# The cross-attention stage of a decoder kernel, issued as turns in program order on five queues

## The chip, the core and the metric

The kernel runs on one core of a Trainium2 chip. The core has a matrix engine (PE, with its weight loads PEld), a vector engine (DVE), a scalar engine (ACT), a general engine (POOL) and a queue that issues transfers (SP); each takes its instructions in order, and they wait for one another by semaphores. The metric is the time of one execution on the device, in microseconds (us). Three runs of the kernel before took 3389.67 to 3397.65 us, with a median of 3396.12.

## The reference

A decoder of two layers on 16 sequences of 128 tokens, 1024 wide, each part followed by an addition and a layer norm: a state-space adapter, a cross-attention, a quantised feed-forward, then a causal attention, a recurrent attention decoder and a binary feed-forward. The change touches the end of the first part and the second:

```python
# end of the adapter (h: its 128-wide result), then norm
h = h @ w_up.T + b_up
x = _layernorm(x + (x_init + h))
# cross-attention, x as (b, c = 128 tokens, n = 1024 columns), ctx as (b, c = 128, m = 256)
q = einsum('oc,bcn->bon', Wq, x)
k = einsum('oc,bcm->bom', Wk, ctx)
v = einsum('oc,bcm->bom', Wv, ctx)
attention = softmax(einsum('bcn,bcm->bnm', q, k) / sqrt(128), axis=-1)
out = einsum('oc,bcn->bon', Wskip, x) + einsum('bnm,bcm->bcn', attention, v)
x = _layernorm(x + out)
```

## The kernel before

The stages follow one another; `stage_cross` comes after `stage_hydra` (the adapter) and before `stage_quant` (the quantised feed-forward). Everything is fp32, and a matrix product of this type is two passes on PE.

For each of the 16 sequences b the stage does, in its source:

- `risen(b)`: the adapter's product, 128 x 1024 in two halves (L526), is added to r (L527), which holds 2x + bias. `Rise.fetch` loads x (L500) and makes r on POOL in two instructions (L502, L503). Then `layer_norm`: sums on DVE (L85 to L89), the reciprocal root on POOL (L95), the normalisation on DVE (L102), written over x. The loop asks for x two sequences ahead; x has 4 buffers and r has 3.
- `context(b)`: loads the context (L534), multiplies it with the folded weight of queries and keys, and with that of values (L536, L538); ACT copies both out (L540).
- `attention(x, kv, i)` for each half i of 512 columns: energies in two pairs (L551), in a ring of three PSUM banks; DVE takes the maximum of each pair (L553) and scales it (L554); ACT makes exponentials and their sums (L557); DVE inverts the sums (L559); POOL multiplies (L560).
- `attended(x, kv, i, ex, r)`: PE transposes the weights (L568), ACT and DVE copy one half each (L570, L572), PE adds the skip product (L575) and the values' products (L577), DVE adds x (L579).
- a second `layer_norm` writes the result over x, and ACT's queue stores it (L597).
- `piece(b)`: one or two of 20 pieces of the next stage's weights: SP loads a chunk (L636, two buffers), ACT rounds it (L621), POOL takes the difference (L622). The first 16 chunks are 128 x 512, the last four 128 x 1024. Sequences 3, 7, 11 and 15 have two pieces each.

The loop issues the next sequence's `risen` and `context` ahead of the second half of the current one. The tile framework schedules these instructions itself: it chooses the order on each queue by priority, and nothing in this stage fixes it. `Ctx.ordered` (L43) fixes it elsewhere: it links each instruction of the engines named to the one before it on the same engine, in the order in which the source issued them. `stage_quant` uses it for four engines, `decoder_scan` for five.

The loads of the next stage (weights L778, x L60) stand on SP's queue behind this stage's, and the weights' space is that of the stage's own buffers.

Of the kernel before, what the change touches and what calls it, by code (L numbers as in the profile page):

```python
# [14 lines left out]
AF = mybir.ActivationFunctionType  # L15
ALU = mybir.AluOpType
AX = mybir.AxisListType
# [6 lines left out]
P = 128  # L24
NB = 16
# [73 lines left out]
def layer_norm(K, pool, src, dst):  # L99

    mv, ve = norm_sums(K, pool, src)
    K.nc.vector.tensor_scalar(dst, src, mv[:, 0:1], norm_root(K, pool, ve), ALU.subtract, ALU.mult)  # L102
# [372 lines left out]
class Rise:  # L475
# [14 lines left out]
    def fold(self, bank):  # L490
# [3 lines left out]
        w["kq"] = K.t(self.pool, [P, P], "wkq")  # L494
        nc.scalar.copy(w["kq"], pw)

    def fetch(self, b):
        K, nc = self.K, self.K.nc
        x = K.t(self.pool, [P, HID], "x", bufs=4)
        nc.sync.dma_start(x, K.a["x"][b])  # L500
        r = K.t(self.pool, [P, HID], "r", bufs=3)
        nc.gpsimd.tensor_tensor(r, x, self.bup, ALU.add)  # L502
        nc.gpsimd.tensor_tensor(r, x, r, ALU.add)  # L503
        self.got.append((x, r))


def stage_cross(K, rise, xmid, dst, piece):

    nc, a = K.nc, K.a
    scale = 1.0 / math.sqrt(128.0)
    w = rise.w
    with ExitStack() as st:
        work = K.pool(st, "c_work", 2)
        ps = K.pool(st, "c_ps", 1, PSUM)

        def risen(b):

            x, r = rise.got[b]  # L520
            if b + 2 < NB:
                rise.fetch(b + 2)
            for i in range(2):
                cols = slice(i * 512, (i + 1) * 512)
                pu = K.t(ps, [P, 512], "pu")
                nc.tensor.matmul(pu, xmid[:, b * P:(b + 1) * P], w["up"][:, cols], start=True, stop=True)  # L526
                nc.vector.tensor_tensor(r[:, cols], pu, r[:, cols], ALU.add)  # L527
            layer_norm(K, work, r, x)
            return x

        def context(b):

            cx = K.t(work, [P, DC], "cx", bufs=3)
            nc.sync.dma_start(cx, a["ctx"][b])  # L534
            pk = K.t(ps, [P, 2, DC], "kv")
            nc.tensor.matmul(pk[:, 0, :], w["kq"], cx, start=True, stop=True)  # L536
            for mc in range(2):
                nc.tensor.matmul(pk[:, 1, mc * P:(mc + 1) * P], cx[:, mc * P:(mc + 1) * P], w["v"], start=True, stop=True)  # L538
            kv = K.t(work, [P, 2, DC], "kv_s")
            nc.scalar.copy(kv, pk)  # L540
            return kv

        def attention(x, kv, i):

            ex = K.t(work, [P, 4, DC], "ex")
            sm = K.t(work, [P, 4], "sm")
            for h in range(2):
                pe = K.t(ps, [P, 2, DC], "e", bufs=3)
                for j in range(2):
                    m = 4 * i + 2 * h + j  # L550
                    nc.tensor.matmul(pe[:, j, :], x[:, m * P:(m + 1) * P], kv[:, 0, :], start=True, stop=True)  # L551
                nm = K.t(work, [P, 2], "nm")
                nc.vector.tensor_reduce(nm, pe, AX.X, ALU.max)  # L553
                nc.vector.tensor_scalar(nm, nm, -scale, None, ALU.mult)  # L554
                for j in range(2):
                    m = 2 * h + j
                    nc.scalar.activation(ex[:, m, :], pe[:, j, :], AF.Exp, bias=nm[:, j:j + 1], scale=scale, accum_out=sm[:, m:m + 1])  # L557
            rs = K.t(work, [P, 4], "rs")
            nc.vector.reciprocal(rs, sm)  # L559
            nc.gpsimd.tensor_tensor(ex, ex, rs.unsqueeze(2).to_broadcast([P, 4, DC]), ALU.mult)  # L560
            return ex

        def attended(x, kv, i, ex, r):
            at = K.t(work, [P, 2, 4, P], "at")
            for mc in range(2):
                pt = K.t(ps, [P, 4, P], "t", bufs=2)
                for j in range(4):
                    nc.tensor.transpose(pt[:, j, :], ex[:, j, mc * P:(mc + 1) * P], K.ident)  # L568
                if mc == 0:
                    nc.scalar.copy(at[:, 0], pt)  # L570
                else:
                    nc.vector.tensor_copy(at[:, 1], pt)  # L572
            cols = slice(i * 512, (i + 1) * 512)
            po = K.t(ps, [P, 512], "o")
            nc.tensor.matmul(po, w["skip"], x[:, cols], start=True, stop=False)  # L575
            for mc in range(2):
                nc.tensor.matmul(po, kv[:, 1, mc * P:(mc + 1) * P], at[:, mc].rearrange("p a b -> p (a b)"),  # L577
                                 start=False, stop=(mc == 1))
            nc.vector.tensor_tensor(r[:, cols], po, x[:, cols], ALU.add)  # L579


        x, kv = risen(0), context(0)
        ex = attention(x, kv, 0)
        for b in range(NB):
            r = K.t(work, [P, HID], "ro")
            for i in range(2):
                if i == 0 and b + 1 < NB:
                    x1, kv1 = risen(b + 1), context(b + 1)
                nxt = None
                if i == 0:  # L590
                    nxt = attention(x, kv, 1)
                elif b + 1 < NB:
                    nxt = attention(x1, kv1, 0)
                attended(x, kv, i, ex, r)
                ex = nxt
            layer_norm(K, work, r, x)
            nc.scalar.dma_start(dst[b], x)  # L597
            piece(b)
            x, kv = (x1, kv1) if b + 1 < NB else (None, None)

# [16 lines left out]
def parts(K, hi, lo, v, eng):  # L619

    K.nc.scalar.copy(hi, v)  # L621
    eng.tensor_tensor(lo, v, hi.bitcast(F32), ALU.subtract)  # L622


def quant_weights(K, slab, stage):

    nc, a = K.nc, K.a
    w, todo = {}, []
    for n, k, m in (("gate", 8, FFI), ("up", 8, FFI), ("down", 4, HID)):
        w[n] = [K.t(slab, [P, k, m], f"w_{n}{i}", F32R) for i in range(2)]  # L630
        todo += [(n, c, m) for c in range(k)]

    def piece(b):
        for n, c, m in todo[b * len(todo) // NB:(b + 1) * len(todo) // NB]:
            raw = K.t(stage, [P, m], "raw")
            nc.sync.dma_start(raw, a[f"ff_w_{n}T"][c * P:(c + 1) * P, :])  # L636
            parts(K, w[n][0][:, c, :], w[n][1][:, c, :], raw, nc.gpsimd)
    return w, piece


def quant_vectors(K, keep):
# [669 lines left out]
class Front:  # L1311
# [131 lines left out]
    def biased(self, t, q):  # L1443
        sl = slice(q * 256, (q + 1) * 256)
        self.nc.vector.tensor_tensor(self.x[t][:, sl], self.x[t][:, sl], self.W["la_yyb"][:, sl], ALU.add)
# [19 lines left out]
    def normed(self, t, h):  # L1465
        sl = slice(h * 512, (h + 1) * 512)
        self.nc.vector.tensor_scalar(self.x[t][:, sl], self.r[t][:, sl], self.mv[:, 0:1], self.rs, ALU.subtract, ALU.mult)
# [446 lines left out]
```

## Time and profile before

| what | us |
|---|---|
| median of three runs | 3396.12 |
| the profiled execution, device time | 3398.38 |
| its span, first to last instruction | 3396.6 |
| first product of the adapter in the stage (L526) | 309.9 |
| last normalisation (L102) starts | 584.5 |
| last store issued (L597) | 585.4 |
| loads of the next stage issued (L778, L60) | 588.1 to 593.0 |
| first use of them (ACT, L671) | 600.8 |

The starts of L102 for the adapter's result, by sequence:

| b | 0 | 1 | 2 | 3 | 4 | 5 | 6 | 7 |
|---|---|---|---|---|---|---|---|---|
| us | 318.3 | 326.1 | 346.1 | 366.9 | 385.4 | 405.4 | 428.0 | 442.9 |

| b | 8 | 9 | 10 | 11 | 12 | 13 | 14 | 15 |
|---|---|---|---|---|---|---|---|---|
| us | 458.9 | 473.1 | 488.5 | 502.7 | 518.3 | 532.6 | 548.1 | 562.4 |

How to read the profile: it records one execution. A group of instructions is named by its line in the kernel and its engine; "x<-r" means that x is written and r is read. A wait is put down to the semaphore that came last. A matrix product's end is modelled. The granted clock of PE is a share of its full rate.

### The profile page before, as it was taken

The page shows a single profiled execution, that of the slowest core. Times are in us where ns is not written, and L with a number is a line of the kernel's source. Part 1 is how long each engine was busy: PE and PEld are TensorE (multiplying, and loading weights), DVE is VectorE, ACT ScalarE, POOL GpSimd, SP SyncE. Part 2 cuts the span into 40 slices and gives each one's busy share as a digit, 9 for nine tenths or more (in the row PEclk, how much of TensorE's full clock was granted, in tenths as well). Part 3 has the DMA queues.
Part 4 walks back from the last instruction along what each step waited for, and adds up shares of the span by engine and source line. Part 5 has one row for each costly group of instructions (what it writes and reads, how often), then busy time and mean ns, then how long its engine had stood idle before and what let it go on. Part 6 is the DMA issues. An engine that isn't in the chain of part 4 may idle for free.

```text
span 3396.6 us, 62991 instructions
## 1 busy us (share of the span) xinstructions
PE 3080.5 (91%) x24917; PEld 1671.7 (49%) x24917; DVE 1858.2 (55%) x5180; ACT 1443.7 (43%) x3642; POOL 904.3 (27%) x1087
## 2 busy tenths in 40 slices
PE   7887887788899999999998999999999999999998
PEld 3444454677455545555553444444444444444465
DVE  5765686688144544545243455555555555555555
ACT  3443333432032323324123555555555555555533
POOL 3333764566233233332011111111111111111122
PEclk8887899999899999898999999999999999999999
DMA  5001321211410100103312000100010000000144
GB/s 195 1 1 30 110 82 71 80 69 63 151 38 13 50 25 19 44 25 100 99 57 80 11 29 24 30 24 30 24 30 23 24 17 24 17 17 14 32 127 103
DMA packets 97215, 170.22 MB, mean 50 GB/s; under 512 B 14362, under 2 KB 55194, under 8 KB 96922
## 3 DMA queue, kind: packets, MB, share of 16 engines
q1 hardware_dynamic: 92858, 157.10, 14.5%
q10 hardware_dynamic: 4064, 9.11, 0.7%
q8 instruction: 197, 3.23, 0.4%
q14 instruction: 96, 0.79, 0.1%
HBM read 115.83 MB, written 51.64 MB: 49 GB/s over the span
## 4 chain that ended last, share of the span: by engine, by line
PE 61%; ACT 10%; DVE 9%; POOL 6%; issue 4%; DMA 1%; SPq 0%; POOLq 0%; DVEq 0%; ACTq 0%
PE p L841 8%; ACT th L1132 8%; PE s L1223 8%; PE pf L1117 7%; PE p L912 6%; PE p L1060 3%; PE m L1672 3%; PE gq L1259 3%; PE ff L1238 2%; PE t L890 2%; PE s L869 2%; POOL xs L675 2%; PE p L854 2%; PE ff L1136 2%; PE s L1167 2%
## 5 line engine op out<-in xcount | busy, mean ns | idle before, releaser
L1132 ACT ACTIVATE th<-pf 128x512 f32<-128x512 f32 x512 | 264.3, 602 | 277.0 <-PE pf L1117 276.9
L878 ACT ACTIVATE s<-s,nm 128x128 f32<-128x128 f32 x512 | 198.2, 389 | 251.6 <-DVE nm L875 221.4
L1252 POOL COPY hist<-gT 128x16 f32<-128x16 f32 x256 | 42.4, 197 | 935.3 <-DVE gT L1250 935.3
L1223 PE MATMUL s<-hb,aD 128*32 128x256 f32 x4096 | 276.1, 387 | 0.6 <-DVE aD L1211 0.6
L912 PE MATMUL p<-ga_Wo,cT 128*128 128x512 f32 x512 | 228.7, 595 | 0.0
L1205 ACT COPY pf<-enc 128x512 f32<-128x512 f32 x381 | 224.6, 589 | 8.1
L841 PE MATMUL p<-xT,ga_Wq 128*128 128x512 f32 x512 | 226.4, 597 | 0.0
L881 POOL TENSOR_TENSOR s<-s,rs 128x512 f32<-128x512 f32 x128 | 133.1, 1039 | 325.1 <-DVE rs L880 317.3
L1117 PE MATMUL pf<-R,waf 32*128 32x160 f32 x2032 | 181.4, 426 | 33.8 <-DVE R L1275 33.8
L841 PEld LDWEIGHTS p<-xT,ga_Wq 128*128 128x128 f32 x512 | 95.4, 190 | 113.8 <-issue 111.0
L912 PEld LDWEIGHTS p<-ga_Wo,cT 128*128 128x128 f32 x512 | 93.8, 190 | 113.8 <-issue 111.7
L1141 DVE TENSOR_REDUCE nm<-s 128x1 f32<-128x128 f32 x128 | 37.3, 292 | 203.6 <-PE s L1136 203.6
L1223 PEld LDWEIGHTS s<-hb,aD 128*32 128x32 f32 x4096 | 106.8, 109 | 84.2 <-DVE aD L1211 45.7
L1243 ACT ACTIVATE fs<-ff,rx 128x384 f32<-128x384 f32 x127 | 73.9, 582 | 173.1 <-DVE rx L1241 171.5
L1136 PE MATMUL s<-th,vaE 128*32 128x128 f32 x2048 | 109.0, 286 | 36.3 <-ACT th L1132 28.1
L892 DVE COPY pT<-t 128x512 f32<-128x512 f32 x128 | 87.9, 687 | 92.5 <-PE t L890 92.3
L95 POOL TENSOR_TENSOR ln_rs<-ln_ve,neghalf 128x1 f32<-128x1 f32 x64 | 37.8, 595 | 345.0 <-DVE ln_ve L89 345.0
L1117 PEld LDWEIGHTS pf<-R,waf 32*128 32x128 f32 x2032 | 79.4, 182 | 99.3 <-DVE R L1275 74.0
L1136 PE MATMUL ff<-th,vaE 128*32 128x128 f32 x2048 | 109.6, 287 | 16.2
L1060 PE MATMUL p<-xT,qT 128*128 128x512 f32 x256 | 115.8, 606 | 0.3 <-ACT qT L1055 0.2
L913 DVE TENSOR_TENSOR xr<-p,xr 128x512 f32<-128x512 f32 x32 | 22.1, 692 | 168.8 <-PE p L912 168.8
L869 PE MATMUL s<-kT,qT 32*128 32x128 f32 x1024 | 107.7, 312 | 0.0
(394 smaller groups left out, 6787.5 us busy)
## 6 DMA issues: line engine op xcount, KB each, us to landing
x<-x SPq DMA_DIRECT2D x79, 512.0 KB, 3.6
xt<-xT SPq DMA_DIRECT2D x8, 1024.0 KB, 7.4
x<-x ACTq DMA_DIRECT2D x16, 512.0 KB, 2.6
xr<-x SPq DMA_DIRECT2D x16, 512.0 KB, 3.6
x<-xr SPq DMA_DIRECT2D x16, 512.0 KB, 2.6
x<-x SPq DMA_DIRECT2D x128, 64.0 KB, 2.3
xb<-r SPq DMA_DIRECT2D x16, 512.0 KB, 3.0
xb<-xb SPq DMA_DIRECT2D x16, 512.0 KB, 4.0
```

The source lines that it names most:

```text
L841: nc.tensor.matmul(pq, lhsT, xT[:, k].rearrange("p i t -> p (i t)"), start=(k == 0), stop=(k == 7))
L869: nc.tensor.matmul(psc[n][:, r, :], qT[sl, 4 * kc + r, i, :], kT[sl, kc, i, :], start=True, stop=True)
L878: nc.scalar.activation(s[:, r, :], s[:, r, :], AF.Exp, bias=nm[:, r:r + 1], accum_out=sm[:, r:r + 1])
L881: nc.gpsimd.tensor_tensor(s, s, rs.unsqueeze(2).to_broadcast([P, 4, P]), ALU.mult)
L912: nc.tensor.matmul(po, cT[:, k, :], w["o"][h][:, k, :], start=(k == 0), stop=(k == 7))
L1060: nc.tensor.matmul(py, xT[:, k, b % 4, :], ys[:, k, :], start=(k == 0), stop=(k == 7))
L1117: nc.tensor.matmul(pf[:, k, first:first + n].rearrange("p b t -> p (b t)"), lhs[32 * k:32 * k + 32, :], rhs[32 * k:32 * k + 32, 32 * first ...
L1132: nc.scalar.activation(th.rearrange("p i (k t) -> p i k t", t=32), pf[:, :, 4 * g:4 * g + 4, :].rearrange("p k i t -> p i k t"), AF.Tanh)
L1136: nc.tensor.matmul(pe[32 * i:32 * i + 32, :], D["va"][:, 31 - b:63 - b], th[:, i, :], start=False, stop=(g % 2 == 1), skip_group_check=True)
L1205: nc.scalar.copy(pf[:, k], D["enc"][:, k])
L1223: nc.tensor.matmul(pg[32 * i:32 * i + 32, :], aD[:, 4 * g + i, :], D["hb"][:, 4 * g + i, :], start=(g == 0), stop=(g == 3), skip_group_che ...
L1259: nc.tensor.matmul(gq[32 * q:32 * q + 32, :], gT[:, c].rearrange("p e b -> p (e b)"), D["gs"][:, c, q * P:(q + 1) * P], start=False, stop= ...
```

## The change

The stage's helpers are split into steps, and one loop issues them as turns from b = -1 to 16: in turn b, the second energies of sequence b, the adapter's product, norm and context of b + 1, both value products of b, the first energies of b + 1, and what is left of b - 1 (its last addition, sums, norm and store). `K.ordered` then holds this order on PE, DVE, ACT, POOL and SP. The norm's root is written in place. The maxima have 4 buffers instead of 2, the small tiles of the norm 3 instead of 2. The store is issued by SP instead of ACT. `quant_weights` gives two functions: `fetch`, which loads, and `piece`, which rounds; the loads of a turn's piece are issued at the end of the turn before it. x is loaded three sequences ahead, and the context two.

```diff
+    def load_x(self, b):
+        x = self.K.t(self.pool, [P, HID], "x", bufs=4)
+        self.K.nc.sync.dma_start(x, self.K.a["x"][b])
+        self.got.append([x])
+
+    def biased(self, b):
+        self.got[b].append(self.K.t(self.pool, [P, HID], "r", bufs=3))
+        x, r = self.got[b]
+        self.K.nc.gpsimd.tensor_tensor(r, x, self.bup, ALU.add)
+
+    def doubled(self, b):
+        x, r = self.got[b]
+        self.K.nc.gpsimd.tensor_tensor(r, x, r, ALU.add)
...
+        def root(key):
+            nc.gpsimd.tensor_tensor(VE[key], VE[key], K.neghalf, ALU.pow)
+
+        def normed(dst, v, key):
+            nc.vector.tensor_scalar(dst, v, MV[key][:, 0:1], VE[key], ALU.subtract, ALU.mult)
...
+        def maxima(b, i, h):
+            nm = PE[b, i, h, "nm"] = K.t(work, [P, 2], "nm", bufs=4)
+            nc.vector.tensor_reduce(nm, PE[b, i, h], AX.X, ALU.max)
+            nc.vector.tensor_scalar(nm, nm, -scale, None, ALU.mult)
...
+        def weighted(b, i):
+            nc.gpsimd.tensor_tensor(EX[b, i], EX[b, i], SM[b, i].unsqueeze(2).to_broadcast([P, 4, DC]), ALU.mult)
...
-        x, kv = risen(0), context(0)
-        ex = attention(x, kv, 0)
-        for b in range(NB):
-            r = K.t(work, [P, HID], "ro")
-            for i in range(2):
-                if i == 0 and b + 1 < NB:
-                    x1, kv1 = risen(b + 1), context(b + 1)
-                nxt = None
-                if i == 0:
-                    nxt = attention(x, kv, 1)
-                elif b + 1 < NB:
-                    nxt = attention(x1, kv1, 0)
-                attended(x, kv, i, ex, r)
-                ex = nxt
-            layer_norm(K, work, r, x)
-            nc.scalar.dma_start(dst[b], x)
-            piece(b)
-            x, kv = (x1, kv1) if b + 1 < NB else (None, None)
+        order = K.ordered((mybir.EngineType.PE, mybir.EngineType.DVE, mybir.EngineType.Activation, mybir.EngineType.Pool,
+                           mybir.EngineType.SP))
+        context_load(0)
+        context_load(1)
+        rise.load_x(2)
+        piece[0](0)
+        for b in range(-1, NB + 1):
+            now, back, soon, far = 0 <= b < NB, 0 <= b - 1, 0 <= b + 1 < NB, 2 <= b + 2 < NB
+            if back:
+                added(b - 1, 1)
+            if now:
+                energies(b, 1)
+                maxima(b, 1, 0)
+                exps(b, 1, 0)
+                piece[1](b)
+            if soon:
+                rest = rise_half(b + 1, 0)
+            if now:
+                maxima(b, 1, 1)
+                exps(b, 1, 1)
+            if soon:
+                rest()
+            if now:
+                turned(b, 0)
+                copied(b, 0, 0)
+            if back:
+                sums(RO[b - 1], (b - 1, "o"), 1)
+            if soon:
+                sums(R[b + 1], (b + 1, "x"), 0)
+                rest = rise_half(b + 1, 1)
+            if far:
+                rise.biased(b + 2)
+            if soon:
+                rest()
+                sums(R[b + 1], (b + 1, "x"), 1)
+                variance((b + 1, "x"))
+                root((b + 1, "x"))
+                context(b + 1)
+            if now:
+                over(b, 1)
+                copied(b, 0, 1)
+                weighted(b, 1)
+            if soon:
+                normed(X[b + 1], R[b + 1], (b + 1, "x"))
+            if back:
+                variance((b - 1, "o"))
+                root((b - 1, "o"))
+            if now:
+                attended(b, 0)
+                added(b, 0)
+            if soon:
+                energies(b + 1, 0)
+                maxima(b + 1, 0, 0)
+                exps(b + 1, 0, 0)
+            if back:
+                normed(X[b - 1], RO[b - 1], (b - 1, "o"))
+                nc.sync.dma_start(dst[b - 1], X[b - 1])
+            if far:
+                rise.doubled(b + 2)
+            if now:
+                turned(b, 1)
+                copied(b, 1, 0)
+            if soon:
+                maxima(b + 1, 0, 1)
+                exps(b + 1, 0, 1)
+            if now:
+                copied(b, 1, 1)
+                attended(b, 1)
+                sums(RO[b], (b, "o"), 0)
+            if soon:
+                over(b + 1, 0)
+                weighted(b + 1, 0)
+            if 0 <= b and b + 3 < NB:
+                rise.load_x(b + 3)
+            if 0 <= b and b + 2 < NB:
+                context_load(b + 2)
+            if soon and 0 <= b:
+                piece[0](b + 1)
+        order()
...
+    came = {}
+
+    def fetch(b):
+        for n, c, m in todo[b * len(todo) // NB:(b + 1) * len(todo) // NB]:
+            raw = came[n, c] = K.t(stage, [P, m], "raw")
+            nc.sync.dma_start(raw, a[f"ff_w_{n}T"][c * P:(c + 1) * P, :])
+
     def piece(b):
         for n, c, m in todo[b * len(todo) // NB:(b + 1) * len(todo) // NB]:
-            raw = K.t(stage, [P, m], "raw")
-            nc.sync.dma_start(raw, a[f"ff_w_{n}T"][c * P:(c + 1) * P, :])
-            parts(K, w[n][0][:, c, :], w[n][1][:, c, :], raw, nc.gpsimd)
-    return w, piece
+            parts(K, w[n][0][:, c, :], w[n][1][:, c, :], came[n, c], nc.gpsimd)
+    return w, (fetch, piece)
```

## The prediction

> **What bounds the kernel now.** I read the page first (PE busy 91% of the span, but no stage is named there), then the stage alone: it runs from the adapter's first product at 309.9 us to the last store at 585.4. Stretches of 15 us show two regimes (columns: us, then busy us of PE, PEld, DVE, ACT and POOL, granted PE clock, DMA share, GB/s):
>
> ```profile
> 390.00:405.00 15.00, 12.52 (x49) 7.79 (x47) 8.78 (x19) 5.09 (x11) 14.04 (x8) 0.93 0.20 73
> 465.00:480.00 15.00, 14.70 (x59) 9.02 (x58) 13.06 (x29) 6.19 (x23) 9.56 (x7) 1.00 0.22 79
> ```
>
> In the first, POOL is the full engine: the scheduler put all 20 weight pieces ahead, and they are over at 401.6. From sequence 7 on, the norm of the adapter's result (L102) comes at 442.94 and, eight sequences later, at 562.38: 14.93 us each. From sequence 0 (318.26) to 7 it is 17.8 us each. PE's own work for one sequence is 12.8 us, from starts that follow one another at full clock: a 512-column product takes 0.86, a 256-column one 0.43 (adapter 1.72, context 0.86, energies 3.4, skip and values 5.1), eight transposes 0.85 (1.7). So 2 us a sequence are idle even in the good part.
>
> The waits of the stage (engine and line, whom it waited for, us, times, longest) say who is late:
>
> ```profile
> ACT ex L557 <- DVE nm L554: 66.4, 37, 6.3
> DVE x L102 <- POOL ln_rs L95: 24.7, 11, 4.6
> ```
>
> L554 is a scaling of 128x2 numbers. Its durations are 113 ns at least and 2072 at most. The timeline (start, us) shows why:
>
> ```profile
> 412.39 2.35 POOL L502 TENSOR_TENSOR r<-x,bup 128x1024 f32<-128x1024 f32 x1
> 414.81 2.34 POOL L503 TENSOR_TENSOR r<-x,r 128x1024 f32<-128x1024 f32 x1
> ```
> ```profile
> 412.79 1.98 DVE L554 TENSOR_SCALAR nm<-nm 128x2 f32<-128x2 f32 x1
> ...
> 415.28 1.91 DVE L554 TENSOR_SCALAR nm<-nm 128x2 f32<-128x2 f32 x1
> ```
>
> Both end with POOL's instruction (414.77 and 417.19 against 414.74 and 417.15), and DVE's queue stands behind them. L102 is of the same kind. Last, the chain of waits in the good part (start, us):
>
> ```profile
> 472.20 0.82 DVE x L102
> ...
> 473.04 2.61 DMA x<-x
> ...
> 475.73 3.37 DMA x<-x
> ...
> 479.16 1.58 POOL r L502
> ```
>
> The store of one sequence frees the buffer into which x of a later one is loaded, and POOL waits for that.
>
> **The change, part by part.** The instruction counts stay: the same products, reductions, copies and 20 pieces. What changes is the order on five queues, and one store queue. I write one turn with R as zero: the moment at which POOL has the adapter's root of sequence b+1.
>
> *DVE and PE after R.* The norm starts 0.04 later (pair at 442.05) and takes 0.81: 0.85. First energies of b+1 start 0.14 later (as at 459.82): 0.98. The maximum starts 1.17 after them (482.58 to 483.75) and takes 0.60, with its scaling: 2.85. POOL's next is `weighted` of the second half (1.89). Does it take the port before the norm? This is the unknown price of the change. In all eight places where two roots follow one another, the L102 that waits for the first starts 0.07 after the second has begun and still runs its 0.81; where a long instruction follows, there is one row:
>
> ```profile
> 345.67 1.49 POOL L622 TENSOR_TENSOR w_up<-raw,w_up 128x512 fp32r<-128x512 f32 x1
> ```
> ```profile
> 346.11 1.60 DVE L102 TENSOR_SCALAR x<-r,ln_mv,ln_rs 128x1024 f32<-128x1024 f32 x1
> ```
>
> There L102 lost, but POOL had begun 0.44 ahead of it; and POOL, which had met the earlier L102 for 0.37 us, lost only 0.22, so that it wants the port some 0.15 after its start. By that the norm wins at 0.07, and costs POOL about 0.73 instead. The rule of the Trainium skill (SBUF — State Buffer, Who interferes with whom) speaks against the change: the shared port pair is an exclusive lock, whoever issues first holds it for the whole instruction, and here POOL's next instruction is queued ready at the very moment at which DVE must first see the root. Taken so, the norm ends at 1.89 + 0.55 = 2.4, not 0.85. By the row a turn pays nothing, by the rule 1.55 and what follows. I take the row.
>
> So `weighted` ends at 2.58, the root of the finished sequence b-1 at 3.09, its norm at 3.94 (again ahead of POOL's `doubled`). `doubled` (2.35 + 0.75 lost) then ends at 6.15, and the scaling of the second maximum, ready at 4.5, stands behind it until 6.17; so does the copy of the transposed half (6.80), for which the last values wait: PE 6.85 to 7.70. The second energies start there, their first maximum is scaled at 9.54, the exponentials end at 10.6.
>
> *SP.* The store goes from ACT's queue to SP's, and SP now carries, in this order, store of b-1, x of b+3, context, raw piece. x of b+3 takes the buffer of b-1, so it waits for the store to land, and the piece is queued behind it. From the norm at 3.94: store issued and landed 2.7 (473.04 to 475.73), x issued at 6.65, two issues of 0.4 later the piece at 7.45. A piece alone lands in 2.7, one issued 1.7 us behind an x in 3.1 (370.73); for 0.8 us behind x and context I take 3.8, between 2.7 and 4.5 (all 896 KB at the rate between the 256 and 512 KB rows). It lands at 11.25. On ACT its copy (0.63, 0.05 to start) comes next: 11.93. On POOL, 0.05 later, the piece's difference (1.27), then `biased` (2.31), then the root (0.52): 16.07. **A turn is 16.1 us.** Without the wait on the piece, ACT would have been free at 10.6 and the turn 15.4; without any port wait PE's copies would allow 13.8. On ACT the second pair of exponentials stands behind the piece, ends at 12.9, and DVE's reciprocal, copy and norm stand behind that; they are ready at 14.6, before 16.07.
>
> *Sum.* First root at 317.2 as before (316.62 + 0.55). Turn 0 has its inputs: after a table load (1.28 on ACT, as before) `weighted` starts at 323.5, then piece, `biased` and root on POOL (1.89 + 1.27 + 2.31 + 0.52): 329.5. Turn 1 has its loads early, and no norm of b-1 stood ahead of `doubled`: exponentials at 10.3, then 4.7 of copy and POOL as above, 15.0: 344.5. Turns 2 to 12: eight of 16.1 = 128.8, three with two pieces (one more 1.27 on POOL) 17.35 = 52.05. Turn 13 carries a `down` piece: copy 1.05, difference 2.35, landing 0.6 more: 18.2. Turn 14 has no `biased` and no x ahead of its piece (10.6 + 0.05 + 1.05 + 2.35 + 0.55): 14.6. Together 558.15 for the root of sequence 15. Behind it the end is like that of before: last two pieces, `weighted`, transposes, values, norm: 22.05 (before, 562.38 to 584.52: 22.1). The last norm starts at 580.2 instead of 584.52: 4.3 us earlier. What follows (last store, weights, first loads of the next stage) hangs on that store in both. Nothing else pays: buffers for maxima go from 2 to 4, 16 store issues of 0.33 leave an ACT that is busy 6 of 15 us; if that cover goes, they cost at most 5.3 us in all, and here they leave.
>
> The profiled execution took 3398.4 (span 3396.6); minus 4.3 is 3394.1. The median of the runs is 2.3 lower, so 3391.8.
>
> **A second rule.** TensorE: Matmul & The Clock Gate (What's actually happening) has the clock halve after an idle window of some 3.4 us. In the trace the clock is 0.75 to 0.93 in four of the stretches before 420 us and 1.00 from 435 to 585. My turn leaves PE 3.3 us idle, in gaps up to 1.5 us: by the row at 1.00 it keeps its clock. Were the rule to bite, first energies take 3.4 instead of 1.7, of which the maximum sees 0.85 a turn, 10 us in all.
>
> **The rivals.**
>
> *POOL wins the port* (slower). Place: the norm right after each root. It ends at 2.4; energies follow at 2.54; the root of b-1 is done at 3.06 and `doubled` runs to 5.33, ahead of the scaling that is ready at 4.31. So the norm of b-1 ends at 6.16, not 3.94, and the whole SP chain with it: 6.16 + 12.15 = 18.3 a turn. With turn 1 at 346, eight of 18.3, three of 19.55, then 20.4, 16.2, and 22.3 for the end, the last norm comes at 610: 25.4 later, **3421**. It decides as soon as POOL takes the port within 0.07 of its start; a loss at `doubled` alone gives 18.0. Over 16.4 us a turn the stage is slower than before. For it: the L622 row. Against: the eight pairs.
>
> *The pieces and the port don't bind* (faster). If pieces land by 10.6, turns are 15.4: 8.4 less, 3383; if scalings slip between POOL's instructions too, 13.8: 27.6 less, 3364. Centre 3374. For it: the good part of before has 14.9 a sequence in a worse order. Against: SP's queue is strictly behind the store.
>
> *The order is not kept* is no rival of weight: the built order on all five queues is the written one.
>
> **How the numbers follow.** A measurement tells 0.3% (10.2 us) from no change; same is 3386 to 3406. Forecast, 3392 (own range 3384 to 3402): 0.40, of it 0.06 faster, 0.28 same, 0.06 slower. Port lost, 3405 to 3435: 0.38, 0.01 same, 0.37 slower. Fast, 3362 to 3386: 0.22, 0.20 faster, 0.02 same. Sum: 0.26, 0.31, 0.43. With both signs holding much, the range goes to both: 3370 leaves out 0.08, 3428 leaves out 0.09.
>
> **What would show it.** Step by step: the L102 of adapter norms 16.1 us apart in turns with one piece; each 0.81 long and 0.04 behind its root (1.6 to 2.4 means the port was lost); ACT's copy of a piece waiting for its DMA; SP waiting for its store; L554's successor held by `doubled` once a turn. It is wrong if PE stays busy (13 us apart), or if the stretch to the next stage's first load changes by more than a few us.

## The result, and the profile after

The changed kernel takes **3429.2 us** (median of four runs, 3425.77 to 3430.7) against 3396.89 for the kernel before in the same comparison: 1.0098 times, 95% interval 1.0080 to 1.0116. It is slower by about 32 us; the forecast was 3392.

The profiled execution has a span of 3428.0 us, 31.4 more than before. I cut it at two points that both kernels have: the adapter's first product of the stage and the first use of the next stage's loads on ACT. Before, the stretch between them is 309.94 to 600.77, 290.8 us; after, 307.55 to 634.75, 327.2 us: 36.4 longer. What lies outside is 5.0 shorter. The outside part varied by up to 19 us over the executions shown below, whatever the edit, so the length of the stage is a sharper measure than the whole time; it is given for every kernel.

The waits of the changed stage (311 to 620 us; engine and line, whom it waited for, us, times, longest):

```profile
ACT ex L589 <- DVE nm L584: 170.9, 31, 9.1
...
PE e L579 <- DVE ln_mv L548: 41.5, 14, 4.3
```

L584 is the scaling that was L554 before (66.4 us there). PE's wait for L548 is new: L548 is only the last instruction that ended, behind the norm (L556) in DVE's queue. Of SP's own waits in the same stretch, this one belongs to the loads of x (L499):

```profile
SPq L499 <- DMA x<-x: 27.9, 12, 2.7
```

What it waits for, 12 times, is the store that frees the buffer, as the prediction had it. Now the place where the root of the next sequence comes (timeline; start, us, engine, line):

```profile
439.99 0.56 POOL L553 TENSOR_TENSOR ln_ve<-ln_ve,neghalf 128x1 f32<-128x1 f32 x1
...
440.51 1.90 POOL L596 TENSOR_TENSOR ex<-ex,sm 128x1024 f32<-128x1024 f32 x1
440.58 2.37 DVE L556 TENSOR_SCALAR x<-r,ln_mv,ln_ve 128x1024 f32<-128x1024 f32 x1 [0.53 <-POOL ln_ve L553]
...
443.86 2.35 POOL L509 TENSOR_TENSOR r<-x,r 128x1024 f32<-128x1024 f32 x1
...
444.97 1.26 DVE L584 TENSOR_SCALAR nm<-nm 128x2 f32<-128x2 f32 x1
446.15 0.80 DVE L556 TENSOR_SCALAR x<-ro,ln_mv,ln_ve 128x1024 f32<-128x1024 f32 x1
```

POOL's `weighted` (L596) begins 0.07 us before the norm, and the norm takes 2.37 us instead of 0.81: it ends 0.54 after L596. All 15 adapter norms that have `weighted` behind their root take 2.37. Then `doubled` (L509) holds the scaling (L584), which ends at 446.23, 0.02 after `doubled`. The norm of sequence b-1 stands behind that scaling on DVE; it is not in a race of its own here. It starts 5.55 to 5.57 us after the adapter's norm in every full turn. The chain of waits of one turn shows what this norm sets off (start, us, what):

```profile
461.38 2.37 DVE x L556
...
463.89 1.21 PE e L579 x4
...
465.85 1.16 DVE nm L584
467.01 0.73 DVE x L556
...
467.76 2.60 DMA x<-x
...
471.33 3.37 DMA raw<-ff_w_upT
...
474.72 0.63 ACT w_up L723
...
475.42 1.27 POOL w_up L724
...
478.95 0.56 POOL ln_ve L553
...
479.54 2.37 DVE x L556
```

Read it as a circle: norm, energies, maximum, scaling, norm of b-1, its store, SP's next issues, the landing of the weight piece, its copy and difference, `biased`, the root, and the next norm. It closes in 18.16 us. The starts of the adapter's norm are 18.17 to 18.81 apart in the eight turns with one piece, 19.81 to 20.79 with two, and the last norm starts at 618.75 instead of 584.52.

### The profile page after: what moved, and what is told of

It is laid out like the page before. It is cut to its first block, busy times and chain, and to the rows that moved or that the text cites. A ratio compares the mean times of both kernels' runs of the same rounds, so it can differ in the third digit from the quotient of the medians.

```text
span 3428.0 us, 62998 instructions
## 1 busy us (share of the span) xinstructions
PE 3082.9 (90%) x24917; PEld 1674.0 (49%) x24917; DVE 1875.7 (55%) x5180; ACT 1441.3 (42%) x3642; POOL 897.9 (26%) x1087
## 3 DMA queue, kind: packets, MB, share of 16 engines
q1 hardware_dynamic: 95162, 165.49, 14.9%
## 4 chain that ended last, share of the span: by engine, by line
PE 60%; ACT 10%; DVE 9%; POOL 5%; issue 4%; DMA 2%; SPq 0%; POOLq 0%; ACTq 0%; DVEq 0%
PE p L948 8%; ACT th L1239 8%; PE s L1330 7%; PE pf L1224 7%; PE p L1019 6%; PE p L1167 3%; PE m L1779 3%; PE gq L1366 3%; PE ff L1345 2%; PE t L997 2%; PE s L976 2%; PE p L961 2%; POOL xs L782 2%; PE ff L1243 2%; PE s L1274 2%
## 5 line engine op out<-in xcount | busy, mean ns | idle before, releaser
L589 ACT ACTIVATE ex<-e,nm 128x256 f32<-128x256 f32 x128 | 59.5, 471 | 170.9 <-DVE nm L584 170.9
L1243 PE MATMUL ff<-th,vaE 128*32 128x128 f32 x2048 | 109.6, 286 | 16.3
L579 PE MATMUL e<-kv_s,x 128*128 128x256 f32 x256 | 75.2, 446 | 47.2 <-DVE ln_mv L548 41.5
```

The lines of the kernel that those rows point to most:

```text
L1243: nc.tensor.matmul(pe[32 * i:32 * i + 32, :], D["va"][:, 31 - b:63 - b], th[:, i, :], start=False, stop=(g % 2 == 1), skip_group_check=True)
```

## The experiments

Three theories were open. **Port:** the norm's wait behind `weighted` costs the time by itself. **Circle:** the turn is the chain shown above, and what matters is only what shortens it. **Scaling:** the held scaling on ACT's way is what costs. The table has the two kernels and the twelve edits; e1 to e11 are edits of the changed kernel, e12 of the one before. "Turn" is the distance of two adapter norms with one piece and with two, where the pattern is regular (turns 2 to 12). Where the piece stands at the turn's end (e4, e5, e8, e10), the longer distance comes one turn later. "Late" in the rows of before and e12 is the mean from sequence 7 to 15. Ratios are to the kernel before, with their 95% intervals.

| kernel | median us | ratio | stage us | turn, 1 piece | 2 pieces |
|---|---|---|---|---|---|
| before | 3394.9 to 3398.3 | 1 | 290.8 | 14.9 late, 17.8 early | |
| after | 3429.20 | 1.0098 [1.0080, 1.0116] | 327.2 | 18.2 to 18.8 | 19.8 to 20.8 |
| e1 | 3428.26 | 1.0097 [1.0082, 1.0113] | 321.9 | 18.2 to 18.9 | 20.2 to 20.6 |
| e2 | 3435.34 | 1.0116 [1.0100, 1.0132] | 324.5 | six of 17.6, 18.6, 19.6 | 19.1 to 19.9 |
| e3 | 3411.99 | 1.0046 [1.0031, 1.0061] | 303.4 | 16.6 to 16.8 | 18.2 to 19.1 |
| e4 | 3409.64 | 1.0044 [1.0027, 1.0061] | 301.6 | 16.9, once 17.2 | 17.3 |
| e5 | 3410.16 | 1.0043 [1.0024, 1.0062] | 299.9 | 17.1, once 16.8 | 17.1 |
| e6 | 3410.54 | 1.0042 [1.0028, 1.0056] | 307.4 | 17.0 to 17.3 | 18.2 |
| e7 | 3412.12 | 1.0042 [1.0024, 1.0061] | 306.4 | 16.8 late, 16.3 to 25.6 early | |
| e8 | 3375.83 | 0.9938 [0.9917, 0.9959] | 272.6 | 15.3 | 16.1 |
| e9 | 3425.25 | 1.0078 [1.0059, 1.0098] | 321.7 | 18.0 to 18.7 | 19.4 to 20.6 |
| e10 | 3371.07 | 0.9918 [0.9896, 0.9939] | 265.7 | 14.8 | 14.8 |
| e11 | 3426.26 | 1.0080 [1.0062, 1.0099] | 315.8 | 17.6 to 18.0 | 18.9 to 20.4 |
| e12 | 3391.93 | 0.9980 [0.9972, 0.9988] | 281.0 | 14.4 late, 16 to 21 early | |

Before ran in each of the four comparisons; its four medians are given, and each ratio is to the runs of the same comparison.

### e1: the norm of the next sequence ahead of `weighted`

```diff
             if now:
-                over(b, 1)
                 copied(b, 0, 1)
-                weighted(b, 1)
             if soon:
                 normed(X[b + 1], R[b + 1], (b + 1, "x"))
+            if now:
+                over(b, 1)
+                weighted(b, 1)
```

> DVE's reciprocal of the sums moves behind the norm of b+1, so that POOL has nothing ready when it has the root. Cycle theory (a turn is one closed chain: root, norm, first energies, maximum and scaling, norm of b-1, store, load of x, piece, its copy and difference, biased, root; a lost port costs only what it adds to that chain): the norm falls from 2.37 to 0.81 us, but `doubled` now starts right behind the root of b-1 and takes the port from the norm of b-1, which ends 6.4 us after the root as before: turns stay at 18.2 to 18.6, time 3424 to 3431. Port theory (each lost port at the root costs its 1.55 us in each of 14 turns, wherever it falls): 22 us less, 3407.

All adapter norms take 0.81 us now, and the time is that of the changed kernel. The timeline of one turn says where the gain went:

```profile
440.93 0.81 DVE L556 TENSOR_SCALAR x<-r,ln_mv,ln_ve 128x1024 f32<-128x1024 f32 x1 [2.44 <-POOL ln_ve L553]
...
444.37 2.35 POOL L509 TENSOR_TENSOR r<-x,r 128x1024 f32<-128x1024 f32 x1
444.44 2.83 DVE L556 TENSOR_SCALAR x<-ro,ln_mv,ln_ve 128x1024 f32<-128x1024 f32 x1 [0.51 <-POOL ln_ve L553]
```

The same race is lost at the next place: `doubled` begins 0.07 before the norm of b-1, which takes 2.83 and ends 447.27. That is 6.34 after the first norm's start, where the changed kernel has 6.37 (446.95 less 440.58). The circle is as long as before. The port theory, that the adapter's norms cost 22 us by themselves, falls.

### e2: `doubled` at the turn's end

```diff
-            if far:
-                rise.doubled(b + 2)
             if now:
                 turned(b, 1)
...
                 weighted(b + 1, 0)
+            if far:
+                rise.doubled(b + 2)
```

> POOL's `doubled` moves from the middle of the turn to its end, behind `weighted` of the next first half. Cycle theory: the norm of b+1 still takes 2.37, but the first scaling and the norm of b-1 no longer stand behind `doubled`: the norm of b-1 ends 5.3 instead of 6.4 us after the root, 1.1 less in each of 12 turns, 3415. Port theory: nothing changes at the root, 3429. If `doubled` at its new place holds up the scalings of the second energies: slower than 3429.

Most turns became shorter (17.6), but the time did not: 3435.34, 20 over the expectation. The stage is 2.7 us shorter than in the changed kernel and the rest of this execution 10.5 us longer, so half of the miss lies outside the stage and is not explained. Inside it, the moved instruction now holds another scaling, that of the second energies, for 1.90 us (0.17 when free), and the piece's copy comes late behind it.

### e3: both moves

> Both edits together. Cycle theory: the norm of b+1 takes 0.81, the norm of b-1 ends 4.35 us after the root instead of 6.4: turns of 16.5 us with one piece, 25 us less, 3404; more than the two edits give one by one (0 and 14). Port theory: 22 us less, as with the first edit alone, 3407.

Both norms take 0.81 us, and 24 us are gone from the stage. As far as the norms go, this is what my forecast assumed: its turn was to be 16.1 and is 16.6 to 16.8. It is not the forecast's order, since `doubled` stands at the turn's end here. The time, 3412, is 8 above the expectation. The timeline shows the port at work in a third place:

```profile
446.19 2.35 POOL L509 TENSOR_TENSOR r<-x,r 128x1024 f32<-128x1024 f32 x1
446.30 2.26 DVE L584 TENSOR_SCALAR nm<-nm 128x2 f32<-128x2 f32 x1
```

### e4: the piece at the turn's end

```diff
             if now:
-                piece[1](b)
...
                 weighted(b + 1, 0)
+            if now:
+                piece[1](b)
```

> ACT's copy and POOL's difference of a piece move from the head of the turn to its end; the chunk is loaded a turn ahead of that. The norms lose the port as in the changed kernel. Cycle theory: store, load of x and piece leave the chain, the root waits for its sums instead, 1.5 us less in single turns and more in those with two pieces: 25 us less, 3404. Port theory: 3429. A theory that only the extra length of two-piece turns matters: 3 times 1.3 to 2 us, 3424.

Here the piece's copy and difference stand behind the turn's last `weighted`, and SP is no longer in the chain of waits of a turn. The norms keep their 2.37 us, yet 25.6 us leave the stage, and turns with one and two pieces are nearly equal. The wait for the piece was part of what set the turn. What is left in the chain of one turn are the norm and two held scalings:

```profile
469.10 2.37 DVE x L556
...
473.49 1.28 DVE nm L584
...
480.02 0.80 DVE nm L584
...
481.53 0.70 DVE r L538
```

This edit moves three things at once, the landing, ACT's copy and POOL's difference; e6 moves the transfer alone.

### e5: all three moves

> The changed kernel with all three moves: VectorE's part of the second energies of b and its weights behind the norms of b+1 and b-1, the doubled difference at the turn's end, and the piece of the next weights at the turn's end. If the cycle of the turn is what costs (norm, store, load and piece were one part of it, the roots and the doubled difference on GpSimd another), both parts are gone from in front of the root and the norms take 0.81 us; what is left in the way is that the scale of the second energies stands behind the doubled difference or the piece on GpSimd. Then a turn is about 15.95 us (16.85 less 0.9), and the kernel 12 us under the one with the late piece alone: 3398. If only the port of the norm costs, 14 norms of 1.56 us are gone and nothing else: 22 us less than the changed kernel, 3407. If the place of the piece alone matters, the time is that of the kernel with the late piece, 3410.

Missed by 12 us: no better than e3 or e4 alone. The timeline shows the new holder of the circle:

```profile
440.07 2.35 POOL L509 TENSOR_TENSOR r<-x,r 128x1024 f32<-128x1024 f32 x1
440.54 1.90 DVE L584 TENSOR_SCALAR nm<-nm 128x2 f32<-128x2 f32 x1
...
443.58 0.68 DVE L538 TENSOR_TENSOR r<-pu,r 128x512 f32<-128x512 f32 x1
```

With `doubled` and the piece at the end of the turn, the first scaling of the second energies is held for 1.90 us, and with it all that DVE has behind it, the next maximum and the adapter's addition (L538) first. What was won at the norms is paid at the scalings.

### e6: the piece's fetch ahead of the store on SP

```diff
+            if soon and 0 <= b:
+                piece[0](b + 1)
             if back:
                 normed(X[b - 1], RO[b - 1], (b - 1, "o"))
                 nc.sync.dma_start(dst[b - 1], X[b - 1])
...
-            if soon and 0 <= b:
-                piece[0](b + 1)
```

> The changed kernel with one move on SP: the fetch of the piece (8 KB into the staging buffer) stands ahead of the store of sequence b-1 and of the load of x behind it, all else unchanged. If the chain norm of b-1, store, load x, piece, difference, root is the cycle, its middle (2.6 us of store, the load's issue and 3.4 us of landing) falls out, and the next limit is GpSimd's own order: turns of about 17.1 us with one piece and 18.4 with two, some 19 us less than the changed kernel: 3410. If SP's order is not in the cycle (the port of the norm or GpSimd's total is), the time stays at 3429. The norm of the next sequence stays at 2.37 us in either case.

It hit: turns of 17.0 to 17.3 and 18.2, 3410.5. Nothing else differs; the norms still take 2.37. (A piece of 128x512 is a transfer of 256 KB in the trace, not 8 KB.) In the chain of waits the store, the load of x and the landing are gone, and the circle runs through scaling, exponentials and the piece's copy instead:

```profile
464.12 2.38 DVE x L556
...
468.51 1.28 DVE nm L584
...
475.33 0.80 ACT ex L589 x3
...
476.94 1.28 POOL w_up L724
...
480.49 0.56 POOL ln_ve L553
```

This is the one-move test of the forecast's part on SP: the order of the transfers alone is worth 19 us of the 32. It does not say that the races are worth only the other 13: e3 takes 24 us out of the same stage and leaves SP's order as it is.

### e7: the same steps without the fixed order

```diff
-        order()
```

> The changed kernel without the order fence behind each turn: the same steps, in the same program order, but the scheduler may place each step by its own priorities on each engine, as in the kernel before. If the fixed order costs the time (pieces spread over the turns, behind SP's store and GpSimd's roots), it falls back to about the time of the kernel before: 3391 to 3403. If the steps themselves cost it (stores on SP, the second energies split from the first, roots in place), it stays at 3415 or more.

Between the two: 3412, and the stage 15.5 us longer than before's. So neither answer is right alone: some 21 us of the stage's 36.4 go with the fixed order, and the rest with the steps as they are written, even when the scheduler may place them. The chain of its late turns has, one behind the other,

```profile
460.78 1.44 DVE nm L584
...
462.81 1.84 DVE nm L584
```

two held scalings, 3.3 us of a turn of 16.8. In which part the split steps, the store on SP and the buffers caused this order was not tried.

### e8: all three moves, and a scaling that the port doesn't hold

```diff
-            nc.vector.tensor_scalar(nm, nm, -scale, None, ALU.mult)
+            for j in range(2):
+                nc.vector.tensor_scalar(nm[:, j:j + 1], nm[:, j:j + 1], -scale, None, ALU.mult)
```

> The kernel with all three moves, and the scale of the maxima (128x2) done as two 128x1 operations, of which none in the traces so far was held by GpSimd (135 to 156 ns each, against 1.2 to 1.9 us of a held 128x2). If the scale's wait for the port is what is left in the cycle, a turn falls to GpSimd's own sum, about 14.9 us, and the kernel to 14 us under the one with all three moves: 3384. If that wait is not in the cycle, it is the same within 3 us, or a little slower by 32 more instructions. If the 128x1 form is held by GpSimd as well, its rows show 1 us or more, and the time is the same.

The two 128x1 instructions take 0.21 to 0.22 us together and are not held, though they start 0.11 us after a long instruction of POOL:

```profile
469.08 2.36 POOL L509 TENSOR_TENSOR r<-x,r 128x1024 f32<-128x1024 f32 x1
469.19 0.21 DVE L585 TENSOR_SCALAR nm<-nm 128x1 f32<-128x1 f32 x2
```

Against e5 the stage is 27 us shorter and the time 34; it is 0.6% faster than before. What the time gained beyond that lies outside the stage, where the edit changes no instruction, so 27 is the safer figure. Turns are 15.3 where 14.9 were expected, but the time undercut its number (3376 against 3384). The edit brought 27 us or more on top of e5 and not 14: the held scalings were a larger part of e5's circle than I had put down. The circle now runs through POOL and the sums:

```profile
460.62 0.81 DVE x L556
...
461.68 1.89 POOL ex L597
...
469.08 2.37 POOL r L509
...
471.48 0.69 DVE r L538
```

Here `doubled` (L509) ends just ahead of the adapter's addition that reads its result (L538): no port, a dependence.

### e9: the divided scaling alone

> The changed kernel with one edit: the scaling of the maxima (128x2) as two 128x1 operations. If the scaling's wait for the port is what the change costs, every turn loses one wait of 1.0 to 1.3 us, 17 us in all, as the same edit brought 34 us on top of the three moves: 3395 to 3412. If the cycle norm, store, load, piece, root decides, the norm of b-1 still stands behind the doubled difference on GpSimd, so turns stay at 18.2 and the time at 3424 to 3430: the edit is worth something only once the other two parts are out of the way.

Worth 4 us in the time, at the edge of what can be told from nothing (the intervals of e9 and the changed kernel overlap), and turns stay at 18 us and more. The same edit takes 27 us from the stage when the rest of the circle is short (e8 against e5), and 5.5 here. The theory that the scalings alone cost the time falls.

### e10: both roots together, both norms together

```diff
                 root((b + 1, "x"))
                 context(b + 1)
+            if back:
+                variance((b - 1, "o"))
+                root((b - 1, "o"))
...
                 normed(X[b + 1], R[b + 1], (b + 1, "x"))
+            if back:
+                normed(X[b - 1], RO[b - 1], (b - 1, "o"))
+                nc.sync.dma_start(dst[b - 1], X[b - 1])
             if now:
                 over(b, 1)
                 weighted(b, 1)
+            if far:
+                rise.doubled(b + 2)
```

(on top of e8; the four steps leave their later places)

> All three moves and the divided scaling (3376), and GpSimd's order changed once more: both roots one after the other, both norms one after the other on VectorE, and the recip of the second half with its weights behind both, then the doubled difference in the middle of the turn again. The trace of the kernel before this edit has turns of 15.3 us in which the chain runs root, norm, weights 1.89, root, norm, two maxima, weights 1.89, doubled difference 2.36, adapter sums, root. With the edit the doubled difference and one pair of weights leave that chain; GpSimd's own sum is 12.2 us, the products' 13.8. If that chain is the cycle, turns are 13.8 to 14.2 and the kernel about 3357. If PE or ScalarE binds already, it stays at 3376; if the doubled difference in the middle holds up a norm again, norms show 2 us or more and the time is above 3376.

The best kernel of the study: 3371.07, 0.8% under the kernel before. All turns are 14.8 us, with one piece or two. Over e8 it is not told apart (their intervals overlap); the stage is 6.9 us shorter. The turn missed 13.8 to 14.2, and the chain says why:

```profile
460.84 1.07 POOL ln_ve L553
...
463.00 1.90 POOL ex L597
...
464.95 1.09 PE t L604 x8
...
468.62 1.73 PE e L579 x8
...
472.08 1.12 PE pu L535 x2
...
473.22 0.70 DVE r L538
```

In the rows from 460.84 to 464.90 (4.1 us) the transposes of the second half wait for the second root, which is held by the first norm, for the second norm behind it on DVE, and then for `weighted`. From there the chain stays on PE, without a pause, to the end of the adapter's product at 473.20 and its addition. What else could move into that gap was not tried.

### e11: a short instruction in the race

```diff
                 root((b + 1, "x"))
                 context(b + 1)
+            if back:
+                variance((b - 1, "o"))
+                root((b - 1, "o"))
             if now:
                 over(b, 1)
                 copied(b, 0, 1)
                 weighted(b, 1)
             if soon:
                 normed(X[b + 1], R[b + 1], (b + 1, "x"))
-            if back:
-                variance((b - 1, "o"))
-                root((b - 1, "o"))
```

> The changed kernel with one move: the root of b-1 (128x1, 0.55 us) stands ahead of the weights of the second half on GpSimd, so that the norm of the next sequence meets a short instruction instead of a long one 0.07 us after its start. By the eight pairs of the kernel before, a norm wins against a root: all norms 0.81 us. By a lock that any instruction of GpSimd takes at its start, they would end with the root or with the weights: 1.0 us or more. The time in either case: the norm of b-1 then stands behind the doubled difference as before, so turns of 18 us or so and 3420 to 3430; 3392 to 3407 if the norm of the next sequence alone decided.

This is the disputed cost by itself. In turn 0 there is no b-1, so `weighted` still follows the root: the norm comes 0.058 us after its start and takes 2.38. In the 13 full turns after it the root of b-1 follows: the norm comes 0.058 to 0.082 after its start and takes 0.81 each time. The same offset, and the winner depends on what POOL runs. The timeline of one turn:

```profile
442.71 1.42 POOL L553 TENSOR_TENSOR ln_ve<-ln_ve,neghalf 128x1 f32<-128x1 f32 x2
443.29 0.81 DVE L556 TENSOR_SCALAR x<-r,ln_mv,ln_ve 128x1024 f32<-128x1024 f32 x1
...
443.75 2.11 POOL L596 TENSOR_TENSOR ex<-ex,sm 128x1024 f32<-128x1024 f32 x1
```

The two roots take 1.42 together: 0.54 for the free one, 0.91 for the one that met the norm, with a short overlap. `weighted`, which begins while the norm still runs, takes 2.11 instead of 1.89: here POOL is the one that waits. The scaling behind it is then held by `doubled` as in the changed kernel (2.01 us), the norm of b-1 comes after 4.8 instead of 5.6 us, and turns are 17.6 to 18.0: the time moved by 3 us, and its interval overlaps with that of the changed kernel.

### e12: the divided scaling in the kernel before

> The kernel before the change with one edit: the scaling of the maxima (128x2) as two 128x1 operations. Its trace has 66.4 us of ScalarE's exponentials waiting for this scaling in the stage, 37 times. If that wait is on the way there too, 5 to 20 us go: 3377 to 3392. If it is covered, or the scheduler's other choices eat it, the time stays at 3391 to 3403. This tells whether what the best kernel wins against the one before is due to the divided scaling alone or to the order.

0.2% faster than before, with an interval clear of 1. The two expected bands overlap, and 3391.9 lies in both: a little of the wait was on the way, most of it was covered. Late sequences are 14.4 us apart on average instead of 14.9, early ones as uneven as they were. So what e10 has over before is not the divided scaling alone; 0.9918 against 0.9980, with intervals that don't touch, is left for the rest of e10: the written order, the store on SP and the buffers, which were not separated.

## Why the prediction was wrong

**The failed step** is in the part on DVE and PE after R: "By the row a turn pays nothing, by the rule 1.55 and what follows. I take the row." The rule was right. By the row's reading the norm wins at 0.07 us after POOL's start; it lost in 15 of 15 places with offsets of 0.07 to 0.09 us. The norm ended 2.4 us after the root, where the forecast had 0.85.

Two readings led there. The first was eight pairs of roots, a root being 128x1, and e11 shows that pairs of roots say nothing about a 128x1024 instruction. The second was the L622 row: POOL had met a norm for 0.37 us and lost only 0.22, from which I took it to want the port 0.15 after its start. In e11 `weighted` meets the end of a norm for 0.35 to 0.38 us in each full turn and loses 0.21 to 0.24, the same shortfall, yet in turn 0 of that kernel it has the port 0.058 after its start. So that shortfall doesn't tell when POOL takes the port. What the L622 rows did show is that a long instruction of POOL keeps the port: besides the row at 346.11, the norm at 318.26 took 1.13 us under an L622 that had begun 0.69 before it.

The Trainium skill (SBUF — State Buffer, Who interferes with whom) says that whoever issues first has the shared port pair for the whole instruction, and that the order of issue decides, not the shape. This trace agrees for the long instructions: the held norm ends 0.55 after POOL's. It differs for the 128x1 root: in e11, at the same offset, the norm comes second, runs at its full speed, and POOL's instruction is the one drawn out. There the measurement decides. The root does wait for the norm: it ends 0.036 to 0.038 us after the norm's end in all 13 full turns of e11, and likewise in e10, where the norm starts 0.22 after the root. So the records read as if the root needs the port only later than 0.22 after its start; what it does until then no run shows.

The same step failed a second time in one clause: the norm of b-1 at 3.94 was to be "again ahead of POOL's `doubled`". In the changed kernel `doubled` holds the scaling ahead of that norm instead, because the late first norm has moved it there. e1 shows that a loss to `doubled` alone is enough to keep the turn at 18.2 to 18.9 (the prediction put such a loss at 18.0); only with both won (e3) does the turn come near the forecast.

**What was right.** The chain by which a turn closes, store on SP, load of x, piece behind both, copy, difference, `biased`, root, is the chain of the profile after, and e6 confirms it by taking its middle out (turns 17.0 to 17.3 and 18.2, against 17.1 and 18.4 expected). The landing of a 128x512 piece was put at 3.8 us and was 3.4 to 4.3. The rival "POOL wins the port" named the right mechanism and size of a turn: 18.3, measured 18.2 to 18.8; the norm of b-1 was to end at 6.16 and ended 6.4 after the root; from there to the next root 12.15 were put down, and 11.8 passed in the turn shown last.

**The sum.** From the root of sequence 0 to the last norm the forecast had 263.0 us (317.2 to 580.2); the profile has 303.8 (314.98 to 618.75). The 40.8 more lie in:

| term | forecast | measured | more |
|---|---|---|---|
| eight turns with one piece | 128.8 | 147.5 | 18.7 |
| three turns with two | 52.05 | 60.7 | 8.7 |
| turn 0, turn 1 | 12.3, 15.0 | 14.3, 17.2 | 4.2 |
| turn 13, turn 14 | 18.2, 14.6 | 21.2, 17.9 | 6.3 |
| the end | 22.05 | 24.95 | 2.9 |

In e3, where no norm is held, the same stretch is 280.8. By that comparison about 23 of the 40.8 go with the lost races, and about 18 with terms that were too small by themselves; it is a rough one, since e3 has `doubled` elsewhere and a scaling held by it. The shares of single edits can't be added: e4 and e6 take 26 and 20 out of the stage and touch no race. Three of the small terms can be read off. The end was taken from before, but there all pieces were done by then. In the changed kernel the last two `down` pieces keep POOL from 605.98 to 610.6, ahead of the last `weighted` (L596, 610.58). The `down` piece of turn 13 was put down as landing in 4.4 us and took 4.9; that of turn 14 was to have landed by 10.6 after the root and landed 13.1 after it. For turn 0, a scaling of the second energies held for 1.40 us stands on the chain, ahead of the exponentials and the piece's copy on ACT, and was not in my sum. (Turn 1 has a slip as well: its "4.7 of copy and POOL" is 4.83 by its own terms.) The rest over before, 36.0 (3394.1 forecast for the profiled execution, 3430.1 measured), is 38.6 for the later last norm, less about 2.5 for what follows.

**The second rule**, on the granted clock: I said that a turn leaves PE idle in gaps of up to 1.5 us and that its clock holds. The gaps were 2.8 to 4.4 us in most turns, and the clock of the changed stage fell to 0.50 ten times between 320 and 615 us, for 3.4 or 6.8 us each. (Before's clock was also below 1.00 in more stretches than I said: in all five from 345 to 420 us.) After the idle time before 424.51, eight energies took 3.75 instead of 1.97 us:

```profile
424.51 3.75 PE L579 MATMUL e<-kv_s,x 128*128 128x256 f32 x8 [3.28 <-DVE ln_mv L548]
```

The length of one gap doesn't decide. A gap of 2.05 us (before 331.87) was followed by the half clock, gaps of 3.28 (before 367.43) and 3.30 (before 500.71) were not. In all fourteen traces the recorded clock changes only at multiples of 3.41 us from its first record. I cut 310 to 620 us of each trace into these stretches of 3.41 us and took PE's busy share of each at full clock. In the 109 that the half clock followed, PE was busy for 0.47 of the stretch at most; in the 972 that it did not follow, for 0.43 at least. So a stretch need not be idle for the clock to fall, only less than about half busy, and a gap that straddles two stretches can pass. My "gaps up to 1.5 us" was the wrong thing to count.

What it cost is small at the place that closes the circle: the norm of b-1 comes after 5.55 to 5.57 us in slow and fast turns alike, since it stands behind `doubled` in both. Whether it cost anything elsewhere was not separated; in e10, which has no gap over 1.5 us after 317 us, the clock stays at 1.00 from 320 us to the last norm.

**The bounds.** The price of the race had two ends, 16.1 and 18.3 a turn, and I forecast the wrong one, although no row of before showed a norm against a 128x1024 instruction of POOL that had just begun. The range reached from the fast rival to 3428, and the result is 1 us above it: the upper end took the rival's 18.3 but not the shortfalls of the turns with two pieces, the first turns and the end.

## What to carry to other kernels

A nearest row has to be near in the thing that is disputed: here the length of the instruction on the other side of the port, not the offset of the two starts. When a fixed order on several queues makes a loop, follow it round until it closes, and expect that removing one wait moves the wait to the next instruction of the same kind: e1, e2 and e9 gained at most 4 us alone, and together with the piece's place (e8) they gained some 53. Small instructions behind long ones are the ones to look at first: making each 128x2 scaling into two of 128x1 cost 64 more instructions on DVE and took 27 us from the stage once the rest was out of its way.

## What the runs showed of the hardware

- A norm on DVE (128x1024) that starts 0.066 to 0.086 us after a 128x1024 instruction of POOL is held until 0.55 us after that one's end, 15 of 15 times in the changed kernel; in turn 0 of e11, at 0.058, too. Against a 128x1 instruction of POOL at 0.058 to 0.082 it is never held (13 full turns of e11). There the POOL instruction takes 0.91 instead of 0.55 us and ends 0.04 after the norm.
- A `TENSOR_SCALAR` of 128x2 is held as a long one is (up to 2.34 us, in e1, for 0.17 us of work). One of 128x1 never was: none of the 512 scalings in e8, e9, e10 and e12 took over 0.156 us, and 246 of them ran wholly inside a POOL instruction of more than 1.2 us. The same operation in two shapes, and only one waits for POOL.
- The PE clock fell to 0.50 after a stretch of 3.41 us in which PE was busy for less than about 0.45 of the time (at most 0.47 in 109 stretches with the fall, at least 0.43 in 972 without), and it stayed there for 3.41 us or multiples of it.
